# Cross-attention and FFN block: the softmax probabilities of the middle groups are turned by VectorE and through DRAM instead of by TensorE

## The chip, the cores and the metric

The kernel runs on one core of a Trainium2 chip. The metric is the device time of one execution in microseconds, the lower the better. Times come from repeated runs (a median is given) and from one execution taken by the hardware profiler, whose span, rows and waits are shown where they are used.

## The reference

Sixteen sequences of 128 rows by 1024 channels, in float32, pass through one block: cross-attention with grouped heads, then a linear FFN whose weight is a 0/1 matrix, both on a layer-normalised input and both added to the residual.

```python
def xattn(q_in, c):                       # q_in = layernorm(x), c = ctx: (16, 128, 1024)
    Q, K, V = q_in @ Wq + bq, c @ Wk + bk, c @ Wv + bv   # 1024, 256, 256 columns
    # 32 query heads and 8 key/value heads of 32; four query heads share one kv head
    w = softmax(Q K^T / sqrt(32))         # per head, 128 x 128
    return concat(w V) @ Wo + bo
def ffn(x):                               # the last 20% of the channels are weighted -4
    return scale * (concat(x_exc, -4 * x_inh) @ kernel)
x = x + xattn(layernorm(x), ctx)
x = x + ffn(layernorm(x))
```

## The kernel before

**Groups and steps.** The 16 sequences are handled in eight groups of two. Each group has four attention steps, one for each sequence `b` and each half `a` of the kv heads; a step covers four kv heads `i`, each with its four query heads `g`. In this text a head tile is the 128 x 512 block of one `i`: 128 queries on the partitions, and for each of four query heads 128 keys. So a group has 16 head tiles, and the kernel 128.

**What a step does.** `scores` makes the four head tiles in PSUM with 32 small matmuls. For each tile `exponentials` takes the row maxima on VectorE (L525) and the exponentials with their sums on ScalarE (L529), and `divide` normalises on VectorE (L540, L541). The weighted sum needs the keys on the partitions: `turn` therefore transposes the four 128 x 128 blocks on TensorE (L546) into PSUM, and ScalarE copies them out (L548). At the end of the step `weighted` multiplies the four turned tiles with V (L556), and ScalarE copies the result to `yT` (L564).

**Filler.** While a step's softmax runs on VectorE and ScalarE, TensorE works through dense pieces of other work: the output product of the group before (`out_proj`, L607), K and V of the next group (L293), the FFN of the group before (L293, its transposes L646), and Q of the next group (`prep_q`, L396). The q and o products are done with seven block products instead of eight (`seven`), for which sums of blocks of Wq and Wo are made in the first group and kept in DRAM. Their weights come as pieces of 512 KB through a ring of eight buffers: `fetch` (L218) asks for the next piece as one is used up.

**What sets the order.** The schedule is written out by hand. A `Stream` holds generators of dense work, each `yield` giving its estimated microseconds, and timed events (`later`). `run(until)` emits events that are due and pieces in turn until the model time is reached. The engines then execute in exactly this order, each in its own queue and each waiting for what it needs. Nearly all DMAs are issued from SP's queue, also in this order. `attend` sets the events of a step: tile `i` begins at 0.7 + 2.4 i us after the scores, its divide comes 2.3 us later, its turn at half of the step's `length` less 3. The main loop gives `length`: 17.4 in the first group, 24.0 or 22.0 in the middle ones. The last group has a loop of its own with steps of 15.

**The start.** The context is transposed by VectorE in 32 x 32 blocks (L319), which needs the channel order on the partitions to be that of `wk_sb` and `wv_sb`. So the context and these two weights are loaded in four DMAs each, one for 32 partitions (L156, L162), half on SP's and half on ScalarE's queue, before TensorE can begin.

Of the kernel before, what the change touches and what calls it, by code (L numbers as in the profile page):

```python
# [22 lines left out]
class Stream:  # L23
# [28 lines left out]
    def run(self, until, keep=lambda: False):  # L52

        while self.now < until or keep():
            while self.events and min(self.events)[0] <= self.now:
                self.fire()
            if not self.piece():
                if not self.events:
                    return
                self.fire()  # L60
# [22 lines left out]
def kernel(  # L83
# [67 lines left out]
    def load_ctx(b, queues=(nc.sync,)):  # L151
        c_t = work.tile([P, NB, NC, 32], FP, tag="ctx", name=f"ctx{b}", bufs=2)
        src = key_value[b].rearrange("(t r) (k c f) -> k r t (c f)", r=32, k=NB, c=NC)
        for k in range(NB):
            dst = c_t[k * 32 : (k + 1) * 32].rearrange("r t c f -> r t (c f)")
            queues[k % len(queues)].dma_start(out=dst, in_=src[k])  # L156
        cs[b] = c_t

    def load_by_quadrants(dst, w, queues):
        src = w.rearrange("(k c f) n -> k f c n", k=NB, f=32)  # L160
        for k in range(NB):
            queues[k % len(queues)].dma_start(out=dst[k * 32 : (k + 1) * 32], in_=src[k])  # L162
# [22 lines left out]
    load_by_quadrants(wv_sb, Wv, two)  # L185
    load_ctx(1, two)
    load_by_quadrants(wk_sb, Wk, two)
# [126 lines left out]
    def turn_ctx(b, h):  # L314
        grp, j = b // GB, b % GB
        if (grp, h) not in cTs:
# [4 lines left out]
            src[:, :, h * HC : (h + 1) * HC],  # L321
# [200 lines left out]
    def exponentials(b, a, i, tile_):  # L522
# [3 lines left out]
        p = work.tile([P, NG, S], FP, tag="p", name=f"p_{n}", bufs=4)  # L526
        total = small.tile([P, NG], FP, tag="total", name=f"total_{n}")
        for g in range(NG):
            nc.scalar.activation(  # L529
                p[:, g],  # L530
                tile_[:, g],
# [4 lines left out]
        return p, total  # L536

    def divide(b, a, i, p, total):
        inv = small.tile([P, NG], FP, tag="inv", name=f"inv_{b}_{a}_{i}")
        nc.vector.reciprocal(inv, total)  # L540
        nc.vector.tensor_mul(p, p, inv.unsqueeze(2).to_broadcast([P, NG, S]))  # L541

    def turn(b, a, i, p):
        tp = ps_tp.tile([P, NG, S], FP, tag="tp", name=f"tpp_{b}_{a}_{i}")
        for g in range(NG):
            nc.tensor.transpose(tp[:, g], p[:, g], ident)  # L546
        pt = work.tile([P, NG, S], FP, tag="pt", name=f"pt_{b}_{a}_{i}", bufs=4)
        nc.scalar.copy(pt, tp)  # L548
        return pt

    def weighted(b, a, pts):

        mm = ps_tp.tile([P, NG, S], FP, tag="tp", name=f"av_{b}_{a}")
        for i in range(NI):
# [4 lines left out]
                rhs=pts[i],  # L559
# [4 lines left out]
        nc.scalar.copy(yTs[b, a], mm)  # L564
# [3 lines left out]
    def out_proj(grp):  # L568
# [12 lines left out]
        def run():  # L581
            b0 = grp * GB
            half = {f"a{j + 1}{a + 1}": yTs.pop((b0 + j, a)) for j in range(GB) for a in range(NA)}
            s = {n: work.tile(S4, FP, tag="comb", name=f"s{n}_{grp}", bufs=4) for n in range(1, 5)}

            def sum_(n, left, right, op):
                left = s[left] if left in s else half[left]
                right = s[right] if right in s else half[right]
# [3 lines left out]
            for us, *args in (  # L592
                (1.0, 1, "a22", "a21", ADD),
                (2.5, 2, 1, "a11", SUB),
                (7.0, 3, "a11", "a21", SUB),
                (9.5, 4, "a12", 2, SUB),
# [5 lines left out]
            def product_of(prod, mm, start):  # L602
                lhsT = half[prod.split()[0]]
# [65 lines left out]
    def attend(b, a, length):  # L669


        tiles = scores(b, a)
        stream.now += 1.2
        pts = [None] * NI
        for i in range(NI):

            def first(i=i):
                p, total = exponentials(b, a, i, tiles[i])
                stream.later(2.3, lambda: divide(b, a, i, p, total))

                def third():
                    pts[i] = turn(b, a, i, p)
                    return 0.45

                stream.later(length / 2 - 3.0, third)

            stream.later(0.7 + 2.4 * i, first)
        return pts
# [48 lines left out]
    with tc.manual_schedule():  # L737
# [56 lines left out]
        def sums_of_wq(k):  # L794
            def then():
                for _ in range(4):
                    fetch()
                if k == 1:
                    spread(combine("o", 1, o_parts[1]), 2.5)
# [10 lines left out]
        for grp in range(NGRP):  # L810
# [4 lines left out]
            length = 17.4 if first else 24.0 if grp < NGRP - 2 else 22.0  # L815
# [17 lines left out]
            elif more:  # L833
# [6 lines left out]
                    mixed(prep_v(nxt), chain(ffn_transpose(p0), ffn_transpose(p1)), 1, 2),  # L840
                    once(get_x, nxt * GB + 1, 5.0),
# [14 lines left out]
            if not more:  # L856
                for q in range(2 * NA):
                    b, a = grp * GB + q % GB, q // GB
                    start = stream.now
                    pts = attend(b, a, 15.0)  # L860
                    stream.later(15.0, lambda b=b, a=a, pts=pts: weighted(b, a, pts) or 1.0)
# [70 lines left out]
```

## Time and profile before

| | us |
|---|---|
| median of 3 runs | 819.83 (819.57 to 819.86) |
| the profiled execution's own time | 817.83 |
| span of its instructions | 816.1 |
| TensorE busy | 789.8 |
| VectorE busy | 459.9 |
| ScalarE busy | 332.7 |
| moved by DMA | 165.14 MB, 202 GB/s over the span |

Busy times add up the lengths of an engine's instructions without counting overlaps twice. A row of the page's groups names line, engine, operation and tiles, then how many there were, their busy time and the mean length of one, then the engine's idle time ahead of them and what ended it. "PE" is TensorE, "PEld" its weight loads, "DVE" VectorE, "ACT" ScalarE, "POOL" GpSimd, "SPq" the queue of the sync engine, from which DMAs are issued. In a table of windows each row gives the stretch, its length, the busy time and the count of instructions of each engine, the granted TensorE clock, the mean busy share of the 16 DMA engines (packets that wait for each other can take it above 1) and GB/s.

### The profile page before, as it was taken

The page shows a single profiled execution, that of the slowest core. Times are in us where ns is not written, and L with a number is a line of the kernel's source. Part 1 is how long each engine was busy: PE and PEld are TensorE (multiplying, and loading weights), DVE is VectorE, ACT ScalarE, POOL GpSimd, SP SyncE. Part 2 cuts the span into 40 slices and gives each one's busy share as a digit, 9 for nine tenths or more (in the row PEclk, how much of TensorE's full clock was granted, in tenths as well). Part 3 has the DMA queues.
Part 4 walks back from the last instruction along what each step waited for, and adds up shares of the span by engine and source line. Part 5 has one row for each costly group of instructions (what it writes and reads, how often), then busy time and mean ns, then how long its engine had stood idle before and what let it go on. Part 6 is the DMA issues. An engine that isn't in the chain of part 4 may idle for free.

```text
span 816.1 us, 13885 instructions
## 1 busy us (share of the span) xinstructions
PE 789.8 (97%) x5216; PEld 593.4 (73%) x5216; DVE 459.9 (56%) x862; ACT 332.7 (41%) x1281; POOL 69.6 (9%) x109
## 2 busy tenths in 40 slices
PE   3997999999999999999999999999999999999998
PEld 3886884678947797488965889568894779756556
DVE  1369748554475554755456454765348565467442
ACT  0243854444334443345333544344434454366200
POOL 1000003002000020000300002000200002000300
PEclk9999999999999999999999999999999999999999
DMA  9999598715885178741887328780578307761511
GB/s 202 357 319 317 198 399 326 210 52 182 273 269 164 43 238 274 262 130 44 286 269 253 80 103 280 276 242 29 179 262 281 132 27 274 246 215 69 195 62 77
DMA packets 81075, 165.14 MB, mean 202 GB/s; under 512 B 5969, under 2 KB 42833, under 8 KB 81009
## 3 DMA queue, kind: packets, MB, share of 16 engines
q1 hardware_dynamic: 79200, 162.55, 59.6%
q10 hardware_dynamic: 1664, 1.57, 1.1%
q8 instruction: 41, 0.67, 0.3%
q0 software_dynamic: 144, 0.14, 0.1%
q14 instruction: 26, 0.20, 0.1%
HBM read 147.46 MB, written 16.78 MB: 201 GB/s over the span
## 4 chain that ended last, share of the span: by engine, by line
PE 86%; DMA 6%; DVE 3%; issue 2%; SPq 1%; ACT 1%; POOL 0%; ACTq 0%; DVEq 0%; POOLq 0%
PE o_u L607 14%; PE f L293 14%; PE q_u L396 12%; PE o_v L607 7%; PE tpp L546 6%; PE q_v L396 6%; PE k L293 5%; PE v L293 5%; PE sc L513 4%; PE av L556 4%; PE o_c L607 3%; PE q_c L396 3%; DMA wo<-in_L_xattn_Wo_dram 2%; PE tp_f L646 2%; PE tp_x L310 1%
## 5 line engine op out<-in xcount | busy, mean ns | idle before, releaser
L529 ACT ACTIVATE p<-sc,negm 128x128 f32<-128x128 f32 x512 | 181.1, 369 | 155.9 <-DVE negm L525 82.3
L548 ACT COPY pt<-tpp 128x512 f32<-128x512 f32 x128 | 74.8, 590 | 117.1 <-PE tpp L546 116.6
L525 DVE TENSOR_REDUCE negm<-sc 128x4 f32<-128x512 f32 x128 | 87.3, 683 | 39.8 <-PE sc L513 39.8
L293 PE MATMUL f<-wf_sb,x2l 128*128 128x512 f32 x256 | 106.0, 414 | 0.0
L529 ACT ACTIVATION_READ_ACCUMULATOR p<-sc,negm 128x1 f32 x512 | 105.8, 207 | 0.0
L293 PE MATMUL f<-wf_sb,x2h 128*128 128x512 f32 x256 | 101.2, 396 | 0.0
L541 DVE TENSOR_TENSOR p<-p,inv 128x512 f32<-128x512 f32 x128 | 88.6, 692 | 4.4
L546 PE MATMUL tpp<-ident,p 128*128 128x128 f32 x512 | 76.7, 273 | 6.3 <-DVE p L541 4.0
L546 PEld LDWEIGHTS tpp<-ident,p 128*128 128x128 f32 x512 | 61.7, 141 | 28.1 <-issue 20.0
L396 PE MATMUL q_u<-t,piece 128*128 128x128 f32 x672 | 81.2, 276 | 0.0
L396 PEld LDWEIGHTS q_u<-t,piece 128*128 128x128 f32 x672 | 78.0, 192 | 0.2 <-DMA piece<-q 0.2
L293 PE MATMUL v<-wv_sb,cT 128*128 128x256 f32 x256 | 62.6, 387 | 12.3 <-DMA wv_sb<-in_L_xattn_Wv_dram 12.3
L178 POOL TENSOR_TENSOR x<-x,bo_b 128x256 f32<-128x256 f32 x64 | 48.8, 795 | 180.2 <-DMA x<-in_x_dram 160.1
L293 PEld LDWEIGHTS v<-wv_sb,cT 128*128 128x128 f32 x256 | 47.5, 195 | 17.7 <-issue 12.3
L607 PE MATMUL o_u<-piece,yT 128*128 128x512 f32 x128 | 59.1, 603 | 0.0
L607 PE MATMUL o_u<-piece,s 128*128 128x512 f32 x128 | 59.0, 594 | 0.0
L607 PE MATMUL o_v<-piece,s 128*128 128x512 f32 x128 | 59.0, 594 | 0.0
L293 PE MATMUL k<-cT,wk_sb 128*128 128x256 f32 x256 | 57.0, 380 | 0.0
L293 PEld LDWEIGHTS f<-wf_sb,x2l 128*128 128x128 f32 x256 | 48.1, 188 | 11.4 <-issue 1.1
L293 PEld LDWEIGHTS f<-wf_sb,x2h 128*128 128x128 f32 x256 | 48.3, 189 | 10.0 <-issue 0.5
L293 PEld LDWEIGHTS k<-cT,wk_sb 128*128 128x128 f32 x256 | 48.5, 190 | 9.0 <-issue 2.6
L564 ACT COPY yT<-av 128x512 f32<-128x512 f32 x32 | 18.7, 585 | 88.0 <-PE av L556 88.0
(77 smaller groups left out, 949.8 us busy)
## 6 DMA issues: line engine op xcount, KB each, us to landing
piece<-o SPq DMA_DIRECT2D x64, 512.0 KB, 4.4
piece<-q SPq DMA_DIRECT2D x56, 512.0 KB, 4.4
piece<-in_L_xattn_Wq_dram SPq DMA_DIRECT2D x50, 512.0 KB, 4.8
piece<-in_L_xattn_Wo_dram SPq DMA_DIRECT2D x48, 512.0 KB, 4.5
xn<-in_x_dram SPq DMA_DIRECT2D x16, 512.0 KB, 5.4
x<-in_x_dram SPq DMA_DIRECT2D x16, 512.0 KB, 4.9
ctx<-in_ctx_dram SPq DMA_DIRECT2D x60, 128.0 KB, 5.9
out_dram<-x SPq DMA_DIRECT2D x15, 512.0 KB, 2.7
```

Source lines behind the costliest of these rows:

```text
L178: lambda cut=cut: nc.gpsimd.tensor_add(x_t[:, cut], x_t[:, cut], bo_b[:, cut]) and None,
L293: nc.tensor.matmul(mm, lhsT=lhsT, rhs=rhs, start=k == 0, stop=k == n - 1)
L396: nc.tensor.matmul(mm if part is None else mm[:, part], lhsT=lhsT, rhs=rhs, start=start and n == k == 0, stop=k == len(some) - 1, skip_gro ...
L513: nc.tensor.matmul(tiles[i][:, g], lhsT=qT[rows, g], rhs=kT[rows, a, cols], start=True, stop=True,)
L525: nc.vector.tensor_reduce(negm, tile_, AX.X, ALU.max, negate=True)
L529: nc.scalar.activation(p[:, g], tile_[:, g], AF.Exp, bias=negm[:, g : g + 1], accum_out=total[:, g : g + 1],)
L541: nc.vector.tensor_mul(p, p, inv.unsqueeze(2).to_broadcast([P, NG, S]))
L546: nc.tensor.transpose(tp[:, g], p[:, g], ident)
L548: nc.scalar.copy(pt, tp)
L556: nc.tensor.matmul(mm[i * HD : (i + 1) * HD], lhsT=vs[b][:, h * HD : (h + 1) * HD], rhs=pts[i], start=True, stop=True,)
L564: nc.scalar.copy(yTs[b, a], mm)
L607: nc.tensor.matmul(mm, lhsT=lhsT[:, 2 * k + c], rhs=w[:, c], start=start and k == c == 0, stop=k == c == 1, skip_group_check=True,)
```

## The change

In the first and the last group the probabilities are turned by TensorE as before. In groups 1 to 6:

- After the divide, VectorE transposes the head tile in place in 32 x 32 blocks (`turn_blocks`). The blocks themselves are then still in the wrong places. Tiles of a pair `i`, `i + 1` lie together, and when the second is done the pair is written to DRAM by one DMA from SP. 4.5 model us later four DMAs from SP (`fetch_blocks`) bring it back, one for each 32 keys, so that each block lands on the partitions of its keys. All of it has one buffer: `p_all` before, `pT_all` after, `p_dram` in DRAM.
- The weighted sums of a step are emitted 4.2 model us into the next step, as an event among the filler. The steps have a length of 21.5 in groups 1 to 5 and of 19.6 in group 6.
- `out_proj` takes its blocks of `yT` when they are first used, and the order and times of its sums change, since one of the blocks is made after it has begun.

Beside that, Wv and Wk are each loaded by one DMA from SP with eight whole rows a partition; the context's channels are assigned to partitions to match, so its turn reads elements that lie eight apart. The first group's four steps get lengths of their own, the second half of the sums of Wo comes later there, and one of the loads of x moves between the two FFN transposes. `Stream.run` now returns when its time is reached and only events are left.

```diff
-                if not self.events:
+                if not self.events or not (self.now < until or keep()):
                     return
...
-        c_t = work.tile([P, NB, NC, 32], FP, tag="ctx", name=f"ctx{b}", bufs=2)
-        src = key_value[b].rearrange("(t r) (k c f) -> k r t (c f)", r=32, k=NB, c=NC)
+        c_t = work.tile([P, NB, 32, NC], FP, tag="ctx", name=f"ctx{b}", bufs=2)
+        src = key_value[b].rearrange("(t r) (k n) -> k r t n", r=32, k=NB)
...
-    load_by_quadrants(wv_sb, Wv, two)
+    nc.sync.dma_start(out=wv_sb, in_=Wv.rearrange("(p c) n -> p c n", p=P))
     load_ctx(1, two)
-    load_by_quadrants(wk_sb, Wk, two)
+    nc.sync.dma_start(out=wk_sb, in_=Wk.rearrange("(p c) n -> p c n", p=P))
...
         nc.vector.transpose(
             cTs[grp, h][:, :, j * S : (j + 1) * S].rearrange("p c (t n) -> p t c n", t=NB),
-            src[:, :, h * HC : (h + 1) * HC],
+            src[:, :, :, h * HC : (h + 1) * HC].rearrange("p t f c -> p t c f"),
         )
...
+    NK, NP = S // HD, NI // 2
+    p_all = const.tile([P, NI, NG * S], FP, name="p_all")
+    pT_all = const.tile([P, NP, NK, 2, NG * HD], FP, name="pT_all")
+    p_dram = dram.tile([NP, NK, P, 2 * NG * HD], FP, name="p_dram")
...
+    def turn_blocks(i):
+        p = probabilities(i, True).rearrange("p g t k -> p t g k")
+        nc.vector.transpose(p, p)
+        if i % 2 == 1:
+            pair = p_all[:, i - 1 : i + 1].rearrange("p i n -> p (i n)")
+            nc.sync.dma_start(
+                out=p_dram[i // 2].rearrange("t p n -> p t n"),
+                in_=pair.rearrange("p (t n) -> p t n", t=NK),
+            )
+            stream.later(4.5, lambda: fetch_blocks(i // 2))
+
+    def fetch_blocks(pair):
+        for t in range(NK):
+            nc.sync.dma_start(
+                out=pT_all[t * HD : (t + 1) * HD, pair].rearrange("r k i n -> r k (i n)"),
+                in_=p_dram[pair, t].rearrange("(k r) n -> r k n", r=HD),
+            )
...
-                rhs=pts[i],
+                rhs=pT_all[:, i // 2, :, i % 2],
...
-                (1.0, 1, "a22", "a21", ADD),
-                (2.5, 2, 1, "a11", SUB),
-                (7.0, 3, "a11", "a21", SUB),
-                (9.5, 4, "a12", 2, SUB),
+                (2.0, 3, "a11", "a21", SUB),
+                (5.6, 1, "a22", "a21", ADD),
+                (6.0, 2, 1, "a11", SUB),
+                (10.0, 4, "a12", 2, SUB),
...
+                def by_vector():
+                    divide(b, a, i, total, blocks)
+                    turn_blocks(i)
+
+                if blocks:
+                    stream.later(2.3, by_vector)
+                else:
+                    stream.later(2.3, lambda: divide(b, a, i, total, blocks))
+                    stream.later(length / 2 - 3.0, by_tensor)
...
-                    spread(combine("o", 1, o_parts[1]), 2.5)
+                    stream.later(8.0, lambda: spread(combine("o", 1, o_parts[1]), 3.0))
...
-            length = 17.4 if first else 24.0 if grp < NGRP - 2 else 22.0
+            length = 21.5 if grp < NGRP - 2 else 19.6
...
-                    mixed(prep_v(nxt), chain(ffn_transpose(p0), ffn_transpose(p1)), 1, 2),
-                    once(get_x, nxt * GB + 1, 5.0),
+                    mixed(
+                        prep_v(nxt),
+                        chain(
+                            ffn_transpose(p0),
+                            once(get_x, nxt * GB + 1, 5.0),
+                            ffn_transpose(p1),
+                        ),
+                        1,
+                        2,
+                    ),
...
+                if first:
+                    length = (17.4, 22.4, 16.0, 14.0)[q]
+                pending = attend(b, a, length if first else None)
+                if first:
+                    stream.run(start + length - 2.0)
+                    stream.run(stream.now, lambda: pending)
+                    weighted(b, a)
+                    stream.now += 1.0
...
+                    stream.run(start + length)
+                if not first:
+                    stream.later(4.2, lambda b=b, a=a: weighted(b, a) or 1.0)
```

## The prediction, made before the result was known

> **What bounds the kernel now.** I read the page first, then windows of one middle group after another, then TensorE's timeline inside such a group, then the DMA side.
>
> ```profile
> PE 789.8 (97%) x5216; PEld 593.4 (73%) x5216; DVE 459.9 (56%) x862; ACT 332.7 (41%) x1281; POOL 69.6 (9%) x109
> ...
> PE 86%; DMA 6%; DVE 3%; issue 2%; SPq 1%; ACT 1%; POOL 0%; ACTq 0%; DVEq 0%; POOLq 0%
> ...
> L548 ACT COPY pt<-tpp 128x512 f32<-128x512 f32 x128 | 74.8, 590 | 117.1 <-PE tpp L546 116.6
> L546 PE MATMUL tpp<-ident,p 128*128 128x128 f32 x512 | 76.7, 273 | 6.3 <-DVE p L541 4.0
> ```
>
> The chain of work is TensorE's. The windows of whole middle groups say it more sharply (columns: length, busy time of each engine, clock, DMA share, GB/s):
>
> ```profile
> 222.54:320.08 97.54, 97.54 (x666) 74.18 (x665) 55.52 (x104) 40.53 (x158) 8.20 (x12) 1.00 0.59 195
> 320.08:417.61 97.53, 97.53 (x665) 74.17 (x665) 55.20 (x104) 40.53 (x158) 8.32 (x12) 1.00 0.60 195
> ```
>
> TensorE is busy for 97.53 of 97.53 us at full clock, and the waits of TensorE between 222 and 612 us list none. Whatever leaves TensorE's queue there shortens the group one for one; VectorE has 42 us of room and the DMA engines some 40%. The price of one turned head tile stands in TensorE's timeline (start, length):
>
> ```profile
> 330.41 1.88 PE L607 MATMUL o_v<-piece,s 128*128 128x512 f32 x4
> 332.13 0.60 PE L546 MATMUL tpp<-ident,p 128*128 128x128 f32 x4
> 332.56 1.88 PE L607 MATMUL o_v<-piece,s 128*128 128x512 f32 x4
> ```
>
> The four transposes start at 332.13 and the next block at 332.56: 0.43 us, not the 4 x 273 ns of the group's row, whose matmuls overlap.
>
> **Part 1, the transposes leave TensorE.** Groups 1 to 6 have 16 head tiles each: 96 x 0.43 = 41.3 us. From below, the chain's 6% of the span for all 128 tiles is 52 us by its finer table (6.4%), 39 for 96. I take 41.3. The period falls to 97.53 - 16 x 0.43 = 90.65 us. The 96 copies at L548 leave ScalarE (57 us), which waited for TensorE anyway: worth nothing.
>
> **Part 2, the weighted sums move.** The same eight matmuls run, but inside the filler and no longer directly ahead of the scores; one more change of operands costs 0.10 us (a block of o matmuls ends its 3.43 us of pace at 342.46, the sums begin at 342.56). 24 x 0.10 = +2.4 us.
>
> **Part 3, VectorE turns.** The nearest row is the turning of the context, same shape:
>
> ```profile
> L319 DVE STREAM_TRANSPOSE cT<-ctx 128x512 f32<-128x512 f32 x32 | 22.0, 698 | 13.4 <-DMA ctx<-in_ctx_dram 13.4
> L541 DVE TENSOR_TENSOR p<-p,inv 128x512 f32<-128x512 f32 x128 | 88.6, 692 | 4.4
> ```
>
> 16 x 0.70 = 11.2 us a group: 55.5 becomes 66.7 of 90.65 us, 74%. It lies beside TensorE, except through the chain of Part 5. The divide writes the same elements in shorter runs: 692 ns kept, with 0 to +0.2 us as bounds. The context's own turn now reads single elements 32 bytes apart. No row shows such a read; L319 reads runs of 32 and takes 0.70. Against the change speaks the Trainium skill, "SBUF — State Buffer", section Specifications (TRN2): lines are 16 bytes, two hits a line are needed for full bandwidth, and each crossing costs. Every element would be a crossing. If that doubled the turn (my estimate, the page gives no factor), two of them ahead of the last softmax of a group's first step would add 1.4 us to Part 5's chain, 8 us over six groups. I take 0.70, the row's, and keep the 8 us for the range.
>
> **Part 4, the start.** TensorE waits 12.3 us for Wv. Until then everything arrives in pieces of 32 partitions; later loads span 128:
>
> ```profile
> 8.00:10.00 2.00, 0.00 (x0) 0.00 (x0) 0.00 (x0) 0.00 (x0) 0.00 (x0) 1.00 1.10 171
> 36.00:38.00 2.00, 2.00 (x11) 1.77 (x10) 0.00 (x0) 0.37 (x1) 0.00 (x0) 1.00 1.04 385
> ```
>
> Wv, whole, is 1.05 MB at 385 GB/s = 2.7 us where at about 200 it took 5.2. Ahead of or beside it go the first context (0.52 MB) and half of the second (0.26 MB) at about 210: 3.7 us. From 2.1 us on that gives 8.5: 3.8 us earlier, with 2.5 and 5 as bounds; Wk then lands before it is needed. The DMA engines are full up to 66 us (share 1.0 and more), so the rest of that stretch moves with it. -3.8 us. The first group's new step lengths and the later sums of Wo meet about 5 us of TensorE waits between 70 and 82 us: 0 taken, bounds -4 and +2. The other scheduling edits (lazy blocks of the next product, sums in another order, x fetched between two transposes) add no instruction: 0; the sums' cover is that the second of two products (3.43 us each) still runs when they are needed.
>
> **Part 5, the new path from VectorE to the weighted sum.** A pair of tiles is written (512 KB), waited for by SP, fetched in four DMAs of 128 KB, and must be there when TensorE, in order, reaches the sums. Everything behind them on TensorE waits too. Rows:
>
> ```profile
> q<-piece SPq DMA_DIRECT2D x8, 512.0 KB, 5.7
> ctx<-in_ctx_dram SPq DMA_DIRECT2D x60, 128.0 KB, 5.9
> out_dram<-x SPq DMA_DIRECT2D x15, 512.0 KB, 2.7
> ```
>
> Take a group's first step, where VectorE is fullest. From the end of its scores (320.0 us) the last divide ends after 13.1 us (333.1). Four turns at VectorE's pace of 0.61 make it 15.5. The write lands in 2.7 us on a quiet queue, 5.7 behind pieces; this step's share is 0.88, so I take 4.5. Here the Trainium skill, "DMA: Bandwidth & Descriptors", section Anatomy of one DMA, would give 2.0 us + bytes/436e3 = 3.2 (an estimate; its fit is for DMAs that GpSimd issues): no wait at all by it, but the busy row is nearer. Then four issues at 0.65 (eight context loads issue within 5.16 us) = 2.6, and the last lands 4.2 to 6.6 later (the range of the context loads at 348 us), 4.2 taken. Sum: 15.5 + 4.5 + 2.6 + 4.2 = 26.8. TensorE reaches the sums one step (22.65) and one product (3.43) later: 26.1. So 0.7 us late, 1 taken: 6 x 1 = +6 us. Ends: 1.1 early (nothing) and 4.8 late (29 us in all). In the other steps the last divide ends after 11.4 to 12.6 us, and about 2 us of margin is left.
>
> SP's own queue: 40 more issues a group, about 20 us of its time, and now two waits a pair, for VectorE's turn and for the write. The pieces of Wq and Wo are queued behind both. A piece is issued when its slot comes free, eight pieces (four products, 13.7 us) ahead of use, and lands after 4.5, so 9 us of delay are covered; with that cover gone each further us would be TensorE's.
>
> **Sum.** 817.83 - 41.3 + 2.4 - 3.8 + 6 = 781.1 against the profiled execution. The median of the runs is 2.0 above it: **783**.
>
> **Rivals.** *Fetched too late (faster, but by less).* The 4.8 us end of Part 5, in each middle group: 783 + 6 x 3.8 = 806. For it: the margin is computed at 0.7 us and the first step falls into the busy DMA stretch. Against it: a stall lets DMAs and VectorE catch up, so it does not add up over steps.
>
> *The DMA engines become the bound (slower).* Now a group moves 195 x 97.5 = 19.0 MB at share 0.59 = 57.5 us. The change adds 16 x 2 x 256 KB = 8.39 MB. At the start's rate of about 200 GB/s for all of it that is 42 us: 99.5 a group, above the old 97.53. Six groups +12, start -3.8, and so 819.83 + 8 = 828. It decides below about 210 GB/s, and its place is the stretch from the q to the o products, where the pieces already need
>
> ```profile
> 330.00:333.00 3.00, 3.00 (x12) 1.52 (x11) 2.93 (x7) 1.55 (x9) 0.00 (x0) 1.00 0.88 289
> 390.00:393.00 3.00, 3.00 (x50) 1.92 (x48) 1.29 (x2) 0.58 (x1) 1.30 (x2) 1.00 1.01 358
> ```
>
> Against it: 0.88 is the pace that TensorE asks for, since 385 GB/s and more go through at 1.04. By bytes the old traffic is 49 us; the writes, spanning 128 partitions as the stores of out do, are 4.19 MB at some 320 = 13, the fetches at 200 are 21: 83 of 90.65 us. In the stretch's 41 critical us I count 31 us of old transfers and 15 of new: 5 behind, under the 9 us of cover.
>
> **How the numbers follow.** Likeliest, TensorE stays the bound with small waits: 0.50, 768 to 792, 783 within it. Its floor is 817.83 - 41.3 - 5 - 4 + 2 = 769.5, rounded down; its top adds the 8 us of Part 3. Fetched too late: 0.29, 792 to 810. DMA-bound: 0.21, of which 0.03 lands within 0.2% of before (1.6 us, what a measurement can tell) and 0.18 above. The range takes the first two: 768 to 810. Faster 0.79, same 0.03, slower 0.18.
>
> **What would show it.** Right: middle groups of about 91 to 92 us, L546's group down to 128 matmuls, the turn of p at 0.70 us, VectorE near 67 us a group, first matmul near 8.5 us, DMA share above 0.8. Wrong: waits of TensorE for the fetched probabilities above 2 us a group (first rival), for pieces (second), or a group longer than 97.5 us.

## The result, and the profile after

The changed kernel takes **884.71 us** (median of 4 runs, 879.30 to 886.97) against 819.7 for the kernel before on the same chip: ratio **1.0788 (95%: 1.0743 to 1.0833)**, 65 us slower. The prediction was 783, with 768 to 810 as its range, so both the direction and the range were wrong. Executions of one kernel can fall into a faster and a slower state; ratios compare the faster ones, and only experiment 3 has slower ones, 875.20 and 877.96 us. The profiled execution of after took 886.97 us, its span 885.0, its mean granted clock was 0.966.

The page of after, its busy times, the chain that ended last by engine, and the groups that the change touches:

```profile
PE 800.4 (90%) x4832; PEld 573.9 (65%) x4832; DVE 537.0 (61%) x958; ACT 277.5 (31%) x1185; POOL 67.7 (8%) x109
...
PE 51%; DMA 25%; DVE 12%; SPq 6%; issue 4%; ACT 2%; POOL 0%; DVEq 0%; POOLq 0%; ACTq 0%
...
L594 PE MATMUL av<-pT_all,v 128*32 128x512 f32 x256 | 58.8, 635 | 48.4 <-DMA pT_all<-p_dram 46.4
L573 DVE STREAM_TRANSPOSE p_all<-p_all 128x512 f32<-128x512 f32 x96 | 68.3, 711 | 3.3
...
p_dram<-p_all SPq DMA_DIRECT2D x48, 512.0 KB, 3.7
pT_all<-p_dram SPq DMA_DIRECT2D x192, 128.0 KB, 4.8
```

TensorE has 384 matmuls fewer and is busy 10.6 us longer: part of what is left runs slower, at a lower clock, and the weighted sums, split by waits, take more busy time (both below). The chain was 86% TensorE before; now a quarter of it is DMA, and VectorE and SP stand in it too. The groups say where: the weighted sums (L594) have 46.4 us of idle time ahead of them, ended by the landing of `pT_all`. The table of TensorE's waits has the same as its first line (us in total, times, longest):

```profile
PE av L594 <- DMA pT_all<-p_dram: 46.4, 18, 4.0
PE v L288 <- DMA wv_sb<-in_L_xattn_Wv_dram: 11.6, 1, 11.6
PE o_v L654 <- DVE x L668: 8.4, 5, 1.7
```

Eighteen waits, on average three in each of the six groups. The windows of the four steps of one middle group show which steps they fall in (length, busy time of TensorE, its weight loads, VectorE, ScalarE and GpSimd, clock, DMA share, GB/s):

```profile
232.79:263.02 30.23, 26.08 (x89) 10.81 (x88) 22.41 (x37) 6.41 (x33) 0.55 (x1) 0.94 0.99 312
263.02:288.10 25.08, 23.48 (x134) 17.18 (x133) 16.18 (x32) 9.60 (x39) 1.09 (x2) 1.00 1.02 266
288.10:311.24 23.14, 23.14 (x161) 18.91 (x161) 16.17 (x30) 8.66 (x37) 0.55 (x1) 1.00 0.42 140
311.24:338.56 27.32, 25.25 (x221) 23.18 (x220) 13.42 (x23) 6.41 (x33) 6.07 (x8) 0.94 0.95 286
```

The group takes 105.77 us; it took 97.53 before, and the forecast had it at about 91 to 92. Only the third step, with a DMA share of 0.42 in its window, has no wait. TensorE's timeline at the head of this group (start, length, and in brackets the idle time and what ended it) shows that the wait is not all that a stall costs:

```profile
237.52 1.05 PE L594 MATMUL av<-pT_all,v 128*32 128x512 f32 x4
241.04 1.05 PE L594 MATMUL av<-pT_all,v 128*32 128x512 f32 x4 [2.47 <-DMA pT_all<-p_dram]
242.03 5.38 PE L654 MATMUL o_c<-piece,yT 128*128 128x512 f32 x8
247.25 3.60 PE L654 MATMUL o_u<-piece,s 128*128 128x512 f32 x8
```

After a wait of 2.47 us eight matmuls take 5.38 us, where the eight after them take 3.60. The windows of 1 us there have the clock (the third number from the end) at half:

```profile
242.00:243.00 1.00, 1.00 (x3) 0.50 (x2) 0.25 (x1) 0.87 (x4) 0.00 (x0) 0.52 1.05 418
243.00:244.00 1.00, 1.00 (x3) 0.44 (x2) 0.97 (x2) 1.00 (x8) 0.00 (x0) 0.50 1.03 414
244.00:245.00 1.00, 1.00 (x3) 0.48 (x2) 0.97 (x3) 1.00 (x8) 0.00 (x0) 0.50 1.00 397
245.00:246.00 1.00, 1.00 (x3) 0.31 (x3) 0.78 (x2) 0.53 (x4) 0.00 (x0) 0.77 0.61 242
```

So the clock was at 0.50 for 3.4 us. All 18 waits stand, like this one, between the first four and the last four sums of a step. At 11 of the 18 such a stretch at 0.50, of 3.4 or 6.8 us, begins during the wait or within 1.5 us of its end (the shortest of these waits is 1.97 us); at the other seven waits, of 1.6 to 3.2 us, there is none. What tells them apart in this trace is where a wait falls. The stretches begin on one grid of 3.413 us: those of 163.53, 214.73 and 242.04 us lie 15 and 8 times 3.413 us apart. Cut along this grid, the 11 waits leave TensorE idle for at least 1.97 us within one cell, the seven for at most 1.85. The wait of 1.97 us that ends at 590.11 lies in one cell and is followed by 0.50; the wait of 3.19 us that ends at 776.37 is cut into 1.34 and 1.85 and is not.

A stall therefore has three parts: the wait, the splitting of the sums, and often the clock. In experiment 2 below, with nothing to wait for, a step's eight sums run together, and the next matmul starts 1.00 us after the first of them:

```profile
250.80 1.07 PE L587 MATMUL av<-bo_b,v 128*32 128x512 f32 x8
251.80 7.17 PE L288 MATMUL k<-cT,wk_sb 128*128 128x256 f32 x32
```

In the stall above it starts 4.51 us after (237.52 and 242.03), so 3.5 us are lost, and the eight matmuls behind take 1.8 us longer: 5.3 us in all.

The same holds for the whole run. Experiment 2 has the same number of matmuls, a span of 798.2 us, and on its page

```profile
PE 759.2 (95%) x4832; PEld 555.2 (70%) x4832; DVE 536.5 (67%) x958; ACT 278.0 (35%) x1185; POOL 71.5 (9%) x109
```

In the changed kernel TensorE is idle 45.6 us longer and busy 41.2 us longer, 86.8 us together. Of the 41.2, 22 are at the sums themselves (58.8 us against 36.7), and 19 are at other lines, which fits the lowered clock.

### The profile page after: what moved, and what is told of

Same layout as the page of the kernel before. It is cut to its first block, busy times and chain, and to the rows that moved or that the text cites. A ratio compares the mean times of both kernels' runs of the same rounds, so it can differ in the third digit from the quotient of the medians.

```text
span 885.0 us, 13453 instructions
## 1 busy us (share of the span) xinstructions
PE 800.4 (90%) x4832; PEld 573.9 (65%) x4832; DVE 537.0 (61%) x958; ACT 277.5 (31%) x1185; POOL 67.7 (8%) x109
## 4 chain that ended last, share of the span: by engine, by line
PE 51%; DMA 25%; DVE 12%; SPq 6%; issue 4%; ACT 2%; POOL 0%; DVEq 0%; POOLq 0%; ACTq 0%
DMA pT_all<-p_dram 19%; PE f L288 12%; PE k L288 6%; PE v L288 6%; PE q_u L391 5%; SPq L584 4%; PE av L594 4%; PE o_u L654 3%; PE q_v L391 3%; PE q L288 3%; DVE p_all L559 3%; DMA piece<-o 2%; PE o_c L654 2%; DVE p_all L573 2%; PE o_v L654 2%
## 5 line engine op out<-in xcount | busy, mean ns | idle before, releaser
L541 ACT ACTIVATE p_all<-sc,negm 128x128 f32<-128x128 f32 x512 | 181.2, 374 | 312.4 <-DVE negm L538 193.6
L541 ACT ACTIVATION_READ_ACCUMULATOR p_all<-sc,negm 128x1 f32 x512 | 108.4, 212 | 0.0
L288 PE MATMUL f<-wf_sb,x2l 128*128 128x512 f32 x256 | 105.6, 412 | 0.0
L594 PE MATMUL av<-pT_all,v 128*32 128x512 f32 x256 | 58.8, 635 | 48.4 <-DMA pT_all<-p_dram 46.4
L288 PE MATMUL f<-wf_sb,x2h 128*128 128x512 f32 x256 | 101.1, 395 | 0.0
L559 DVE TENSOR_TENSOR p_all<-p_all,inv 128x512 f32<-128x512 f32 x128 | 89.2, 697 | 4.4
L391 PEld LDWEIGHTS q_u<-t,piece 128*128 128x128 f32 x672 | 86.4, 210 | 8.1 <-issue 8.0
L391 PE MATMUL q_u<-t,piece 128*128 128x128 f32 x672 | 89.8, 295 | 0.0
L288 PE MATMUL v<-wv_sb,cT 128*128 128x256 f32 x256 | 62.1, 392 | 13.3 <-DMA wv_sb<-in_L_xattn_Wv_dram 11.6
L573 DVE STREAM_TRANSPOSE p_all<-p_all 128x512 f32<-128x512 f32 x96 | 68.3, 711 | 3.3
L654 PE MATMUL o_v<-piece,s 128*128 128x512 f32 x128 | 58.8, 598 | 8.4 <-DVE x L668 8.4
L288 PE MATMUL k<-cT,wk_sb 128*128 128x256 f32 x256 | 61.5, 401 | 1.2 <-DVE cT L314 1.2
L288 PEld LDWEIGHTS v<-wv_sb,cT 128*128 128x128 f32 x256 | 49.0, 197 | 20.6 <-issue 11.6
L493 DVE SCALAR_TENSOR_TENSOR qT<-q_u,bqs 128x512 f32<-128x512 f32 x21 | 14.5, 692 | 76.9 <-PE q_u L391 76.9
L594 PEld LDWEIGHTS av<-pT_all,v 128*32 128x32 f32 x256 | 8.6, 109 | 80.1 <-issue 54.0
L288 PEld LDWEIGHTS k<-cT,wk_sb 128*128 128x128 f32 x256 | 51.0, 202 | 14.5 <-issue 3.8
L288 PEld LDWEIGHTS f<-wf_sb,x2l 128*128 128x128 f32 x256 | 48.1, 188 | 17.1 <-issue 7.0
```

What stands on the lines that cost most here:

```text
L288: nc.tensor.matmul(mm, lhsT=lhsT, rhs=rhs, start=k == 0, stop=k == n - 1)
L391: nc.tensor.matmul(mm if part is None else mm[:, part], lhsT=lhsT, rhs=rhs, start=start and n == k == 0, stop=k == len(some) - 1, skip_gro ...
L493: nc.vector.scalar_tensor_tensor(out[c], mm, scale, other, MULT, ADD)
L541: nc.scalar.activation(p[:, g], tile_[:, g].rearrange("p (t k) -> p t k", t=NK), AF.Exp, bias=negm[:, g : g + 1], accum_out=total[:, g : g ...
L559: nc.vector.tensor_mul(p, p, factor)
L573: nc.vector.transpose(p, p)
```

## The experiments

**1 and 2: what is lost to waiting, and what to the traffic.** In both, the weighted sums of groups 1 to 6 read a buffer that is always there (`bo_b`) in place of the turned probabilities, so their values are not those of the reference. In the first, everything else stays, writes and fetches too; in the second the round trip through DRAM is left out as well.

```diff
# both
-                rhs=pT_all[:, i // 2, :, i % 2],
+                rhs=bo_b[:, :HALF]...        # groups 1 to 6
# the second only: in turn_blocks
-            nc.sync.dma_start(out=p_dram[i // 2]..., in_=pair...)
-            stream.later(4.5, lambda: fetch_blocks(i // 2))
```

> Left out: in groups 1 to 6 the weighted sums read a constant (bo_b) in place of the turned probabilities, so nothing waits for the fetch; the write, the four fetches, VectorE's turns and every other instruction stay. Theory (the fetch lands after TensorE has reached the sums; the wait, the lower clock after it and the softmax held behind it are the whole loss): about 785 us, groups of about 91 us, granted clock back at 1.00. Rival 1 (DMA traffic itself is the bound): still about 880. Rival 2 (VectorE has too much, with the context's turn at 1.09 instead of 0.70 us): above 830.

> Left out as in the run without the wait, and also the write to DRAM and the four fetches of each pair. Theory: within 5 us of the run without the wait (780 to 790). Rival 1 (DMA-bound): this one alone drops, to about 785, while the run without the wait stays near 880. Rival 2 (VectorE): no change against the run without the wait, and both above 830.

Measured: 837.67 us (ratio 1.0205, 1.0176 to 1.0233) and 797.65 us (0.9725, 0.9701 to 0.9749). Without the trip the group is 93.28 us, VectorE's turns included:

```profile
246.07:268.49 22.42, 22.42 (x133) 17.01 (x132) 16.07 (x32) 9.59 (x39) 1.09 (x2) 1.00 0.56 158
268.49:291.64 23.15, 23.15 (x162) 18.92 (x161) 16.18 (x30) 8.76 (x37) 0.55 (x1) 1.00 0.23 79
291.64:314.23 22.59, 22.59 (x222) 21.39 (x221) 13.42 (x23) 6.51 (x33) 6.64 (x8) 1.00 0.88 291
314.23:339.35 25.12, 23.36 (x89) 10.01 (x88) 22.12 (x37) 6.39 (x33) 0.55 (x1) 1.00 0.84 280
```

The price put on TensorE's transposes was therefore right: three steps are full at clock 1.00 and two of them under 22.65 us. Waiting for the probabilities costs 884.7 - 837.7 = 47 us net. But the first experiment, which waits for no probabilities, is still 40 us slower than the second, and 53 above the 785 that was expected of it: the trip holds up something else. Its table of TensorE's waits names a new one, which the table of after does not have:

```profile
PE f L288 <- DVE x L711: 27.8, 5, 9.1
```

TensorE waits for VectorE's residual at L711, because it cannot reuse the PSUM of `f` until that is done. VectorE in its turn stands in front of a LayerNorm, as its timeline shows:

```profile
283.49 1.29 DVE L271 BATCH_NORM_STATS2 st_a<-xn 128x6 f32<-128x512 f32 x2 [13.02 <-DMA xn<-in_x_dram]
```

13.02 us of VectorE, waiting for one load of x. SP's timeline has that load last in a queue (start, length of the issue):

```profile
270.53 0.94 SPq L576 DMA_DIRECT2D p_dram<-p_all  x2
275.33 3.65 SPq L584 DMA_DIRECT2D pT_all<-p_dram  x8
279.08 0.38 SPq L162 DMA_DIRECT2D xn<-in_x_dram  x1
```

SP waits for the turned pair, then for the write to land, then issues eight fetches; the load of x, behind all of them in its queue, goes out at 279.08.

**5: that load on another queue.** Experiment 1, and the second load of x of each group is issued from ScalarE's queue.

```diff
-                            once(get_x, nxt * GB + 1, 5.0),
+                            once(get_x, nxt * GB + 1, 5.0, nc.scalar),
```

> As the run without the wait (constant in place of the turned probabilities in groups 1 to 6), and one load of x per group, the one between the two FFN transposes, is issued from ScalarE's queue instead of SP's. Bytes and all other DMAs stay. Theory (that load stood behind SP's wait for a write and held VectorE's queue for 13 us, and TensorE behind it): TensorE's waits for x in the FFN (27.8 us) and the low clock after them go, 838 becomes 800 to 810. Rival (the DMA engines are full, whatever the order): stays within 8 us of 838.

Measured: 802.41 us (0.9795, 0.9778 to 0.9812), 35 us less than experiment 1. The wait at L288 is gone from TensorE's table, whose largest entry behind the start is now

```profile
PE o_u L658 <- DMA piece<-o: 5.0, 5, 1.6
```

and the whole round trip, 50 MB, costs 802.4 - 797.7 = 5 us as long as nobody waits for its data. By their bytes alone the DMA engines are not the bound.

**16: the same move alone.** The changed kernel with only that load on ScalarE's queue.

> Nothing left out. The changed kernel with only the one load of x per group moved to ScalarE's queue. Theory (in the changed kernel the late fetch stops TensorE first, so this load is no limit there): 878 to 888. If the load of x costs by itself: 850 to 870.

Measured: 884.25 us (1.0756, 1.0679 to 1.0833), no change. While TensorE waits for the probabilities, the load of x has time to come. It is a second limit, 35 us deep, that lies hidden under the first.

**3 and 9: sums later.** The weighted sums of a group's first three steps are emitted 9.0 model us into the next step, not 4.2; in experiment 9 with the load of x on ScalarE's queue too. The sums of the last step keep their place.

```diff
-                    stream.later(4.2, lambda b=b, a=a: weighted(b, a) or 1.0)
+                    us = 4.2 if q == 2 * NA - 1 else 9.0
+                    stream.later(us, lambda b=b, a=a: weighted(b, a) or 1.0)
```

> The weighted sums of a group's first three steps are emitted 9.0 instead of 4.2 model us into the next step; the last step's stay at 4.2, since the output product needs them. Nothing is left out. Theory: the three waits within a group go, the one at a group's beginning stays: groups of 97 to 100 us instead of 107, so 830 to 845 in all, and no TensorE wait for the fetch in the three steps. Rival 1: the DMA engines set the pace, so the time stays within 10 us of 885. Rival 2: same, 875 to 885.

> Nothing left out. The run with later sums and, besides, the load of x on ScalarE's queue. Theory: TensorE's waits for x (21 us) and the clock after them go, and the wait for the fetch at a group's beginning stays (12 us and its echo in clock and softmax): 820 to 840. Rival (DMA engines full): within 10 us of the 870 of the run with later sums.

Measured: 853.85 and 864.27 us for experiment 3 (1.0472, 1.0395 to 1.0549; the 870 in the expectation of experiment 9 is the median with the two slower runs), above the 830 to 845 expected, and 832.64 us (1.0164, 1.0130 to 1.0198) for experiment 9. Experiment 9 answers experiment 16: with the waits of three steps out of the way, moving the load of x is worth about 26 us (832.6 against 859.1, the mean of the two). What is left in experiment 9 is the step whose sums were not moved, the last of a group:

```profile
PE av L594 <- DMA pT_all<-p_dram: 19.5, 6, 4.3
```

Six waits, one in each group.

**12: all sums later.** Sums at 9.0 in every step; so that the head of the next group has work to put ahead of them, part of the Q products is left for it. Context, its weights and the load of x as in experiments 4 and 9.

```diff
-                    stream.later(4.2, lambda b=b, a=a: weighted(b, a) or 1.0)
+                    stream.later(9.0, lambda b=b, a=a: weighted(b, a) or 1.0)
...
-                stream.add(once(residuals, grp), prep_x(nxt, 1), qs[nxt])
+                near = []
+                stream.add(
+                    once(residuals, grp), prep_x(nxt, 1), between(qs[nxt], 40, near.append, 1)
+                )
...
-                if q == 2 * NA - 1:
+                if q == 2 * NA - 1 and first:
                     stream.run(start, lambda: stream.queue)
+                elif q == 2 * NA - 1:
+                    stream.run(start, lambda: not near)
```

> Nothing left out. All four steps of groups 1 to 6 are turned by VectorE as in the change, but every weighted sum comes 9.0 model us into the next step; so that the last one is in time for the output product, the last two of seven block products of the next group's Q are left for the beginning of the next group. Context layout and weight loads as before the change, the load of x on ScalarE's queue. Theory (the trip costs nothing once nobody waits for it): no TensorE wait for the fetch, groups of 91 to 93 us, 793 to 806. Rival (the fetch at a group's beginning is late by more than 5 us because the DMA engines are full there): waits remain, 815 to 835.

Measured: 844.25 us (1.0294, 1.0273 to 1.0314), slower than experiment 9 and than the rival's 815 to 835. My expectation failed. TensorE still waits 11 times for the probabilities:

```profile
PE av L599 <- DMA pT_all<-p_dram: 26.7, 11, 4.1
```

Five of these waits (9.7 us) are for the sums of a group's first step, four (13.0 us) for those of its second, two (4.0 us) for those of its last.

For the first step experiment 1 points to the reason. There no wait for the probabilities moves the schedule, so it shows the bare trip of a group's first step, in the stretch where the o pieces, the contexts and x are loaded. Scores end at 221.0 and the last turn at 238.98; SP issues at

```profile
239.80 0.37 SPq L576 DMA_DIRECT2D p_dram<-p_all  x1
244.92 1.76 SPq L584 DMA_DIRECT2D pT_all<-p_dram  x4
246.77 3.77 SPq L213 DMA_DIRECT2D piece<-in_L_xattn_Wq_dram  x3
251.34 2.23 SPq L584 DMA_DIRECT2D pT_all<-p_dram  x4
```

The write of 239.80 lands 11.5 us later (the view of its line alone, L576, around its issue):

```profile
DMA to landing us min/median/max: 11.5/11.5/11.5
```

and only then, at 251.34, do the fetches go out. They land after (the same view of L584)

```profile
DMA to landing us min/median/max: 9.2/9.3/9.3
```

253.4 + 9.2 = 262.6, where the sums stand at 252.1 in the same run: more than 10 us late, and by the same numbers still 5 us late with the sums at 9.0. The windows of that stretch have the DMA share above 1 throughout:

```profile
242.00:246.00 4.00, 3.77 (x9) 1.44 (x8) 3.67 (x5) 0.00 (x0) 0.26 (x1) 1.00 1.05 399
246.00:250.00 4.00, 4.00 (x40) 2.15 (x39) 2.10 (x5) 0.64 (x4) 0.00 (x0) 1.00 1.12 273
```

The length of the landing fits what was queued. From 231.84 us on SP issues nine transfers of 512 KB, this write the last; at the 339 GB/s of the whole step (221.0 to 248.5 us) these 4.7 MB alone take 14 us, to 245.8 (an estimate from the trace), and earlier pieces were still on their way.

For the second step the order on SP's queue delays the write. In experiment 12 the last turn of such a step ends at 257.31 us, but the write of its pair stands in SP's queue behind eight loads of the context and behind the fetch of the pair before:

```profile
255.41 11.02 SPq L156 DMA_DIRECT2D ctx<-in_ctx_dram  x8
266.57 1.76 SPq L589 DMA_DIRECT2D pT_all<-p_dram  x4
268.44 0.38 SPq L581 DMA_DIRECT2D p_dram<-p_all  x1
```

It goes out 11 us after the turn, lands after 6.4 us, and the sums wait 3.47 us.

**4: the context as before.** Layout, loads and turn of the context, and the loads of Wv and Wk by quadrants, as in the kernel before.

```diff
-        c_t = work.tile([P, NB, 32, NC], FP, tag="ctx", name=f"ctx{b}", bufs=2)
+        c_t = work.tile([P, NB, NC, 32], FP, tag="ctx", name=f"ctx{b}", bufs=2)
...
-    nc.sync.dma_start(out=wv_sb, in_=Wv.rearrange("(p c) n -> p c n", p=P))
+    load_by_quadrants(wv_sb, Wv, two)
```

> The changed kernel with the context's layout, its turn (runs of 32 elements) and the loads of Wv and Wk by 32 partitions as they were before the change. Theory: the context's turn falls from 1.09 to 0.70 us, the first step's softmax ends about 0.8 us sooner, and part of each group's first wait goes: 3 to 10 us faster, 875 to 882. Rival 2 (VectorE is what is late): 845 or less. Rival 1: no change.

Measured: 880.9 us (1.0745, 1.0681 to 1.0808), which cannot be told from the changed kernel. The turn of the context itself is another matter. In the changed kernel the group by forms has it at

```profile
L314 DVE STREAM_TRANSPOSE cT<-ctx 128x512 f32<-128x512 f32 x32 | 34.5, 1086 | 11.3 <-DMA ctx<-in_ctx_dram 11.3
```

and here, with the old layout, at

```profile
L319 DVE STREAM_TRANSPOSE cT<-ctx 128x512 f32<-128x512 f32 x32 | 21.8, 692 | 13.0 <-DMA ctx<-in_ctx_dram 13.0
```

Reading elements 32 bytes apart makes it 1.57 times as long. That is real, and it is not where the 65 us went.

**13: does the stall travel over ScalarE?** The copy of the weighted sums to `yT` stands in ScalarE's queue ahead of exponentials. A rival explanation had it that a late sum delays these, then the divides and turns, then the next fetch. Here the copy is put 5.0 model us later for the first three steps.

```diff
+        def copy_out():
+            yTs[b, a] = work.tile(S4, FP, tag="yT", name=f"yT{b}_{a}", bufs=7)
+            nc.scalar.copy(...)
...
+            stream.later(copy_us, copy_out)
```

> Nothing left out. The changed kernel, with the weighted sums where they are; only ScalarE's copy of them to yT is emitted 5.0 model us later in a group's second to fourth step. So TensorE still waits for the fetch, but ScalarE, and with it the exponentials and VectorE, are not held behind it. Theory with the echo (a late sum delays the softmax of its own step and so the next fetch): fewer and shorter waits for the fetch, 885 becomes 860 to 875. Without the echo: 880 to 888.

Measured: 882.4 us (1.0773, 1.0709 to 1.0837), with 46.7 us of waits for the probabilities where the changed kernel has 46.4. The rival falls.

**6, 7, 10, 11: only the steps that have time.** TensorE turns the probabilities of some steps as before, VectorE those of the others, with the sums at 9.0. Experiment 6 leaves the last step of each group to TensorE, experiment 7 the first and the last. Both have the context of experiment 4 and the load of x on ScalarE's queue. Experiments 10 and 11 are 7 and 6 with the sums `s` of the o products in the order and at the times of the kernel before.

```diff
+                plain_turn = first or q not in (0, 1, 2)     # experiment 7: (1, 2)
...
+                pending = attend(b, a, span if plain_turn else None)
...
# 10 and 11 only
-                (2.0, 3, "a11", "a21", SUB),
-                (5.6, 1, "a22", "a21", ADD),
-                (6.0, 2, 1, "a11", SUB),
-                (10.0, 4, "a12", 2, SUB),
+                (1.0, 1, "a22", "a21", ADD),
+                (2.5, 2, 1, "a11", SUB),
+                (7.0, 3, "a11", "a21", SUB),
+                (9.5, 4, "a12", 2, SUB),
```

> Nothing left out. Only the first three steps of groups 1 to 6 are turned by VectorE, their sums 9.0 model us into the next step; the last step is turned by TensorE as before the change; context layout and weight loads as before the change; the load of x on ScalarE's queue. Theory: 72 of 96 tiles leave TensorE (31 us) and no wait for the fetch is left, apart from small ones in the full DMA stretch: 792 to 812. Rival (DMA-bound with three quarters of the traffic): above 830.

> Nothing left out. As the run with three steps, but only the second and third step of groups 1 to 6, where the DMA engines have room, are turned by VectorE. Theory: 48 tiles leave TensorE (20.6 us), no wait for the fetch: 799 to 806. Rival (DMA-bound): about 815 to 825, since only half of the traffic is left and it falls beside few pieces; it can't tell the two apart alone, the pair with three steps does.

> Nothing left out. The run with two steps and, besides, the order and times of the output product's sums as they were before the change, since no block of yT comes late any more. Theory (TensorE's 9.0 us of waits for these sums, and the first step of 26.4 us, come from sums held until 6.0): first step back to about 24.7 us, 817 becomes 804 to 810. Rival (the first step is longer for the traffic of the steps around it): 814 to 818.

> Nothing left out. The run with three steps and, besides, the order and times of the sums as before the change. Theory: TensorE's 17.6 us of waits for the sums go, 826 becomes 800 to 812. Rival (full DMA stretch with traffic in the first step): 820 to 828.

| steps turned by VectorE | sums of o as changed | as before |
|---|---|---|
| 0, 1, 2 | 826.19 (1.0092, 1.0056 to 1.0128) | **803.09 (0.9791, 0.9770 to 0.9813)** |
| 1, 2 | 816.68 (0.9961, 0.9950 to 0.9973) | 805.96 (0.9833, 0.9817 to 0.9848) |

Experiments 10 and 11 came out as expected; 6 and 7 missed their ranges of 792 to 812 and 799 to 806. The waits for the probabilities are down to 1.5 us in experiment 6, but a wait for VectorE's sum `s` has taken their place, and the older order removes that one. The entry in experiment 6's table of TensorE's waits:

```profile
PE o_u L659 <- DVE s L641: 17.6, 7, 2.9
```

In experiment 11's table this entry is gone, and the largest that the trip leaves is

```profile
PE av L599 <- DMA pT_all<-p_dram: 2.9, 3, 1.6
```

Experiment 11 leaves nothing out of the work, and takes 16 us less than the kernel before (819.49 in the same runs). By the price of Part 1 its 72 tiles are worth 31 us; where the other 15 went was not followed up. In it the writes of the first steps land after 3.3 to 3.9 us, where those of experiment 1 take 8.4 to 11.5 in groups 2 to 6. The windows of one first step in experiment 11 and of the one shown above in experiment 1 have DMA shares of 0.91 and 1.06:

```profile
219.50:242.20 22.70, 22.19 (x85) 9.96 (x81) 20.43 (x37) 6.03 (x32) 0.55 (x1) 1.00 0.91 297
221.00:248.50 27.50, 23.97 (x92) 9.73 (x89) 22.32 (x37) 6.39 (x33) 0.55 (x1) 1.00 1.06 339
```

The last step's trip, which would fall into this stretch, is left out there; that this is what makes the room is argued, since other edits differ too.

**14 and 15: the trip on another queue.** Write and fetches are issued from GpSimd's queue, in the changed kernel and in experiment 11, so that SP never waits for them.

```diff
-            nc.sync.dma_start(
+            nc.gpsimd.dma_start(      # the write of the pair and its four fetches
```

> Nothing left out. The changed kernel with the write and the four fetches of each pair issued from GpSimd's queue instead of SP's; everything else, SP's loads in their order included, stays. If the trip is late because it stands behind the pieces in SP's ring and SP's waits: landing falls to below 6 us for writes in the full stretch, SP's waits for p go, TensorE's waits for the fetch fall from 46 us to below 20, and 885 becomes 810 to 850. If the DMA engines are full whatever the queue: 870 or more. A price of its own: GpSimd waits for the write and then gives rstd to VectorE late, up to 20 us.

> Nothing left out. The run with three steps and the old sums (803), with the trip on GpSimd's queue. Own ring decides: its remaining waits (2.9 us for the fetch, and what the late fetches and SP's waits cost in the steps of 24 to 25 us) go, 795 to 801. DMA engines full: 800 to 806. GpSimd held by its waits, and rstd with it: above 808.

Measured: 942.92 us (1.1506, 1.1451 to 1.1561) and 864.33 us (1.0532, 1.0486 to 1.0578), both some 60 us slower than the same kernel with the trip on SP. The issue rows of experiment 14:

```profile
p_dram<-p_all POOLq DMA_DIRECT2D x48, 512.0 KB, 5.2
pT_all<-p_dram POOLq DMA_DIRECT2D x192, 128.0 KB, 7.9
```

The fetches land 7.9 us after issue where SP's landed after 4.8, the writes after 5.2 instead of 3.7, and TensorE waits 84.7 us for the probabilities instead of 46.4. In experiment 15 the medians are 6.5 and 5.7 us against 3.7 and 3.6 in experiment 11. Taking the waits out of SP's order lets its pieces go out undisturbed, and the trip then has to share the engines with them. That last sentence is argued; that the landings are longer is measured. What makes them longer, the sharing or the way in which GpSimd issues, was not separated, nor was how much the order of GpSimd's own work adds. In experiment 15 VectorE's waits for GpSimd's `rstd` do grow, from 22.1 us in experiment 11 to 47.5, the price that the expectation named.

## Why the prediction was wrong, point by point

- **Part 1 and 2, TensorE's price: right.** Three of the four steps of experiment 2 take 22.4 to 23.2 us at full clock; the forecast's mean was 22.65 + 0.1. TensorE is busy 91.5 us in that group; 91.05 were forecast. L565 is down to 128 matmuls.
- **Part 3, VectorE: right for the probabilities, wrong for the context.** The turn of p takes 0.711 us; 0.70 was taken. The context's turn takes 1.086 us, where the row's 0.70 was taken against the rule of the Trainium skill, "SBUF — State Buffer", section Specifications (TRN2). The rule was the better guide: 16-byte lines, one hit a line, and 1.57 times the duration. VectorE is busy 68.2 us in a group, 66.7 were forecast.
- **Part 4, the start: wrong, small.** The first matmul starts at 11.6 us, not 8.5, and group 1 begins at 126.8 (before: 123.8; experiment 2: 125.0). Wv in one DMA gained 0.7 us, not 3.8, and the rest of the first group gave it back.
- **Part 5, the step that failed.** The chain for a group's first step was summed to 26.8 us against a deadline of 26.1. Its terms, as the bare trip of experiment 1 shows them:

| term | predicted | measured |
|---|---|---|
| last turn, after the scores' end | 15.5 | 18.0 |
| from there to the write's issue | 0 | 0.8 |
| write to landing | 4.5 | 11.5 |
| four issues | 2.6 | 2.1 (251.34 to 253.4) |
| last fetch to landing | 4.2 | 9.2 |
| sum | 26.8 | 41.6 |
| TensorE reaches the sums after | 26.1 | 31.1 |

  About 10 us late instead of 1, in that run. Most of it is landing time: 12 of the 15 us of error. Experiment 5, where the load of x is out of the way, confirms that it is not the first term: in its group with scores ending at 314.9 us the last turn comes after 15.7 us, the write lands after 10.8 and the last fetches after 9.4 to 10.0, and the sums would again be some 10 us late. In the changed kernel the stalls themselves stretch the step. In the group shown above the write lands after 4.9 us, near the 4.5 taken, but the last turn comes only after 20.7 us and the last fetches land after 8.3 to 8.5; TensorE, held up before, reaches the sums after 34.9 us and still waits 1.6. From the ends that Part 5 names (5.7 for the write, 6.6 for the fetch) its late end comes to 4.3 us, not 4.8. I chose the middle between a quiet queue and one busy with pieces, for a stretch whose DMA share was already 0.88 and to which 15 us of transfers were to be added: I had counted them myself, for a rival, and did not carry them over to the latency. The estimate of 3.2 us for a pair, by the fit in the Trainium skill, "DMA: Bandwidth & Descriptors", section Anatomy of one DMA, agrees with the landings of a quiet stretch (2.9 and 3.3 us between 300 and 305 us in the changed kernel) and not with the 11.5 us of the full one.
- **"In the other steps about 2 us of margin is left": wrong.** In the middle group shown, the sums of the first, third and last step all wait, 1.6 to 2.5 us each; only those of the second do not. For the third step the turns end 15.4 us after the scores, where the forecast's terms give 13.8 to 15.0; but the last four fetches, issued right behind two loads of x on SP's queue, land 7.4 to 7.7 us after issue instead of 4.2.
- **"A stall does not add up over steps": wrong in its price.** The waits do not grow (longest 4.0 us). But there were 18 of them at 2.6 us each, each split its sums, about 1 us more, and at 11 of them the clock fell, worth 1.8 us in the one shown. The sum had six waits of 1 us, and nothing for the split or the clock.
- **SP's queue: the right worry, the wrong victim.** The 9 us of cover for the pieces held: no wait for pieces above 5.0 us in all in experiment 5. What was caught behind SP's waits was one load of x, with VectorE behind it, then TensorE: 35 us, visible only where the probabilities are not waited for.
- **The rivals.** *Fetched too late* named the mechanism, and was too small by its two prices: it put 3.8 us more on a group where nearly 15 came, and so came out on the wrong side of before. *The DMA engines become the bound* was wrong as put: the traffic alone costs 5 us (experiment 5 against 2), and 8.39 MB a group do go through. Here the full engines cost time through the landings, not through the bytes.

The sum, then: 797.7 without the trip, where the forecast without its 6 us of stall would be 777. Of these 21 us the start explains 5 (1.2 later instead of 3.8 earlier), and the 2.2 us by which a group of experiment 2 is longer than 91.05 another 13, 1.7 of the 2.2 being TensorE's wait for VectorE at the residual of o, `PE o_v <- DVE x`, about once a group; some 2 us stay unplaced. Upon that come 5 us of traffic, and then 82 us up to 884.7. How these are divided depends on the order of taking away: the wait for the probabilities first gives 47 (experiment 1) and the blocked load then 35 (experiment 5), the load first gives nothing (experiment 16) and the wait then all 82. What part of them is lowered clock was not separated by a run of its own; by the mean clocks it is at most 25 us: (1 - 0.966) x 885 = 30 us are missing in the changed kernel, (1 - 0.994) x 799 = 5 in experiment 5.

## What to carry to other kernels

A round trip through DRAM is a chain of landings, and each must be priced at the load of the stretch where it falls, the trip's own traffic included: here 11.5 us for a write in the full stretch, 2.9 to 3.3 in a quiet one. List what is queued behind a wait on the issuing queue, down to the smallest load, and ask who waits for that; a second limit can lie hidden under the first, so take away one wait and look again before judging an edit without effect. And when a change suits some steps and not others, apply it to those: three steps of four, with later sums, the older order of the `s` and one load of x on another queue, gave 0.979 where the change gave 1.079.

## What the runs showed of the hardware that was not expected

- A wait of TensorE of 2.47 us was followed by 3.4 us at a clock of 0.50, and eight matmuls took 5.38 us instead of 3.60. The 18 waits for the probabilities divide by the idle time within one cell of a grid of 3.413 us: 1.97 us and more in the 11 that went with such a stretch, 1.85 and less in the other seven. The length of the wait alone, 1.97 to 4.0 us and 1.6 to 3.2, does not tell.
- A write of 512 KB landed after 2.9 us where the step's DMA share was 0.42, and after 11.5 us where it was above 1.
- Eight weighted sums in one go held TensorE for 1.00 us; with a wait between the fours each four took 1.05 us.
- A VectorE transpose of 128 x 512 fp32 that reads elements 32 bytes apart takes 1.086 us, contiguous runs 0.692.
- The same 50 MB issued from GpSimd's queue landed later than from SP's (7.9 against 4.8 us for the fetches), and the kernel became 58 us slower.
